# First layer of a four-layer image network: 64-row products on row halves, streamed weights, three PSUM double banks

## The chip, the cores and the metric

The kernel runs on one core of a Trainium2 chip. The metric is the device time in microseconds (us) of one execution. The core has a matrix engine (TensorE, in the profile PE, its weight loads PEld), a vector engine (DVE), a scalar engine (ACT), GpSimd (POOL) and a queue engine (SP) that here issues most DMAs.

## The reference

Four layers run one after the other on 8 images of 56 x 56 positions with 192 channels, all in fp32. The change touches the first, whose input is normalised in groups of 6 channels per image (as the kernel lays it out):

```
p = silu(x @ p_w.T + p_b);  q = silu(x @ q_w.T + q_b);  v = silu(x @ v_w.T + v_b)   # 192 -> 576
a1, a2 = rpe_mlp(...) * decay            # Toeplitz coefficients per channel, 2*56 each
qv = q * v
o1 = toeplitz(qv along w, a1);  o2 = toeplitz(qv along h, a2)
out = (p * (o1 + o2)) @ o_w.T + o_b      # 576 -> 192, then added to x
```

Per channel, o1 + o2 is computed as one product of two matrices with 120 rows: image rows beside a 56 x 56 Toeplitz table, for both directions at once. The other three layers (a window attention, a gated unit with attention and a recurrent scan) are the same before and after.

## The kernel before, in words

**Tiles.** In the first layer an image lies with its channels on the partitions: `xa` holds channels 0 to 127 (128 x 3136), and `xb` channels 128 to 191 of the upper half image on partitions 0 to 63 and of the lower half on 64 to 127 (128 x 1568). So every product over 192 channels is one product of 128 rows and one of 64; the 64-row products of the two halves use the two halves of the array's rows. `GroupNormSplit` (L79) measures an image with bn_stats (L115), spreads the means over groups by small products with a group matrix (L98, eight instructions) and settles scale and shift.

**Stages.** An image goes through five stages c = 0 to 4 of 128 channels (64 in the last). The lists of steps that a stage runs are woven together by `merge`, and the order of TensorE's instructions is exactly the order in which the program writes them (`manual_schedule` for PE); the other engines are put in order by the scheduler.

- `project` (L297, L304) computes q and v for the channels of the next stage in four groups of 14 rows. ACT applies silu (L313) and DVE and POOL write q*v twice into `qv`, straight and across (L325, L331).
- `turn_both` and `turn` (L358, L377) transpose `qv` channel rows; DVE copies the result into `ol` and ACT into `or` (L363, L384). A bank of PSUM is free when both have copied.
- `convolve` (L401) multiplies `ol` with `or` channel by channel, and results go to `ot` (L419, L421). Then `toeplitz` (L275) fetches the tables for the channels two steps on, over SP.
- `post` (after stages 1 and 3, run as the `fill` of stages 2 and 4) has seven groups of 8 image rows. `gate` computes p (L442 with 128 rows, L449 with 64) and its silu (L456). `back` transposes `ot` (L467, 120 rows at a time) and DVE multiplies with p (L476). `out` multiplies with o_w, 128 columns wide for the first 128 output channels (L487) and 64 wide for the rest (L492), and DVE adds to the accumulators `acca` and `accb` (L428, L430). `in_turn` runs them as back(g-1), gate(g), out(g-1).
- `post_tail` (fill of the next image's stage 0) does the same for the last 64 channels (L532, L539, L553, L559, L566, L578).
- In stages 0, 2 and 4 the fill runs with the turns; in stages 1 and 3 (and in stage 0 of the first image), which have no fill, the first two projection groups of the next stage do. So three and four turns follow each other there.

**Buffers.** PSUM has eight banks; the first layer uses them as four tiles of two banks, tag "c", in rotation. SBUF work tiles are "s" (128 x 784, four) and "po" (four). The weights of `project` and `post` (`wqv`, `wp`) stay in SBUF for the whole layer.

An fp32 product shows as two MATMUL records, a transposition as one. The form "64*128" in a record gives the rows and columns of the array that it uses.

Of the kernel before, what the change touches and what calls it, by code (L numbers as in the profile page):

```python
# [15 lines left out]
C = 192  # L16
CP = 96
# [36 lines left out]
HH, HQ = H // 2, HW // 2  # L54

# [17 lines left out]

def sub(ap, *dims):

    return bass.AP(ap.tensor, ap.offset, [list(ap.ap[0]), *(list(d) for d in dims)])


class GroupNormSplit:  # L79


    def __init__(self, cx, es, gmat):
        self.cx = cx
        nc = cx.nc
        pool = es.enter_context(cx.tc.tile_pool(name="gs_c", bufs=1))
        self.g = cx.tile(pool, [128, 2, 2, 128], "gmat")
        nc.sync.dma_start(self.g, gmat)
        self.eps = cx.tile(pool, [128, 1], "eps")
        nc.vector.memset(self.eps, EPS)
        self.small = es.enter_context(cx.tc.tile_pool(name="gs_s", bufs=1))  # L90

    def spread(self, bank, v):

        nc = self.cx.nc
        ps = bank()[:, 0:2]
        for m in range(2):
            for k in range(2):
                nc.tensor.matmul(  # L98
                    ps[:, m : m + 1], self.g[:, k, m, :], v[:, k : k + 1], start=(k == 0), stop=(k == 1)
                )  # L100
        return ps

    def steps(self, xa, xb):
# [4 lines left out]
        new = lambda name: cx.tile(self.small, [128, 2], name)  # L108
        mv = cx.tile(self.small, [128, 2, 2], "mv")
        mean, gms, dev = new("mean"), new("gms"), new("dev")  # L110
        parts = [(x, n, cx.tile(self.small, [128, n, 6], f"st{n}")) for x, n in ((xa, 7), (xb, 4))]
# [5 lines left out]
        def deviate(bank):  # L117
            for k, (_, _, st) in enumerate(parts):
                nc.vector.bn_aggr(mv[:, k, :], st.rearrange("p a b -> p (a b)"))
            nc.vector.tensor_copy(mean, mv[:, :, 0])  # L120
            nc.vector.tensor_copy(gms, self.spread(bank, mean))
            nc.vector.tensor_tensor(dev, mean, gms, ALU.subtract)
            nc.vector.tensor_tensor(dev, dev, dev, ALU.mult)
            nc.vector.tensor_tensor(dev, dev, mv[:, :, 1], ALU.add)

        def settle(bank):
            sd, rstd, nbias = new("sd"), new("rstd"), new("nbias")
            nc.scalar.activation(sd, self.spread(bank, dev), AF.Sqrt, bias=self.eps)
# [7 lines left out]
def layer0(cx, xin, xout, w, consts):  # L136
# [11 lines left out]
    T2, T1 = slice(0, H), slice(64, 64 + H)  # L148
    cx.open(B)
    cx.between = ExitStack()  # L150
    with ExitStack() as es:
        gn = GroupNormSplit(cx, cx.between, w["gmat"])
# [3 lines left out]
        wk = es.enter_context(tc.tile_pool(name="l0w", bufs=4))  # L156
        psc = es.enter_context(tc.tile_pool(name="l0a", bufs=4, space=PSUM))
# [4 lines left out]
        def bank():  # L162
            return banks()[:, 0]

        def load_raw(b):
            xa, xb = cx.tile(np_, [CA, HW], "xa"), cx.tile(np_, [128, HQ], "xb")
            image_dma(nc.sync, xin[b], xa, xb)
            return xa, xb
# [5 lines left out]
        wqv = [cx.tile(cp, [128, 9, 128], f"wqv{k}") for k in range(2)]  # L174
        wp = [cx.tile(cp, [128, NC, 128], f"wp{k}") for k in range(2)]
        for k in range(2):
            nc.scalar.dma_start(wqv[k], w[f"w_qv{k}"])
# [62 lines left out]
        for k in range(2):  # L240
            nc.scalar.dma_start(wp[k], w[f"w_p{k}"])
# [41 lines left out]
        def project(xn, c):  # L283


            n = 7 * H
            tail = c == NC - 1
# [4 lines left out]
            def gates(g):  # L292
                pss = [banks() for _ in js]
                for j, ps in zip(js, pss):
                    for h in range(2):
                        at = h * HQ + g * n
                        nc.tensor.matmul(  # L297
                            ps[:, h, 0:n], wqv[0][:, j, :], xn[0][:, at : at + n],
                            start=True, stop=False,
                        )  # L300
                for j, ps in zip(js, pss):
                    for h in range(2):
                        rows = slice(h * CB, (h + 1) * CB)
                        nc.tensor.matmul(  # L304
                            ps[:, h, 0:n], wqv[1][rows, j, :], xn[1][rows, g * n : (g + 1) * n],
                            start=False, stop=True,
                        )
                ts = []
                for i in range(2):
                    j, ps = js[0 if tail else i], pss[0 if tail else i]  # L310
                    rows = slice(i * DS, (i + 1) * DS) if tail else slice(0, 128)
                    t = cx.tile(wk, [128, 2, n], "s")[0 : DS if tail else 128]
# [119 lines left out]
        def post(j, xn, ot, acc):  # L432

            n = 4 * H

            def gate(g):
                ps = banks()
                out = lambda u, h: ps[:, h, u * n : (u + 1) * n]
                for u in range(2):
                    for h in range(2):  # L440
                        at = h * HQ + g * n
                        nc.tensor.matmul(  # L442
                            out(u, h), wp[0][:, 2 * j + u, :], xn[0][:, at : at + n],
                            start=(u == 0), stop=True, skip_group_check=True,
                        )
                for u in range(2):
                    for h in range(2):
                        rows = slice(h * CB, (h + 1) * CB)
                        nc.tensor.matmul(  # L449
                            out(u, h), wp[1][rows, 2 * j + u, :], xn[1][rows, g * n : (g + 1) * n],  # L450
                            start=False, stop=True, skip_group_check=True,
                        )
                sps = []
                for u in range(2):
                    sp = cx.tile(wk, [128, 2, n], "s")
                    nc.scalar.activation(  # L456
                        sp, ps[:, :, u * n : (u + 1) * n], AF.Silu,
                        bias=bp[:, 2 * j + u : 2 * j + u + 1],
                    )
                    sps.append(sp)  # L460
                return sps

            def back(g, sps):
                pt = banks()
                for h in range(2):
                    for i in range(4):
                        nc.tensor.transpose(  # L467
                            pt[:, h, i * 120 : (i + 1) * 120],
                            ot[:, :, h * HH + 4 * g + i],
                            ident[0:120, 0:120],  # L470
                        )
                pos = []
                for u in range(2):
                    po = cx.tile(wk, [128, 2, 4, H], "po")
                    src = pt[:, :, 0:480].rearrange("p h (i c) -> p h i c", c=120)
                    nc.vector.tensor_tensor(  # L476
                        po, sps[u].rearrange("p h (i c) -> p h i c", c=H),
                        src[:, :, :, u * 64 : u * 64 + H], ALU.mult,
                    )
                    pos.append(po.rearrange("p h i c -> p h (i c)"))  # L480
                return pos

            def out(g, pos):
                ps = banks()
                pa, pb = ps[:, 0, 0 : 2 * n].rearrange("p (h i) -> p h i", h=2), ps[:, 1, 0:n]
                for u in range(2):
                    nc.tensor.matmul(  # L487
                        pa, wo[:, 2 * j + u, 0:CA], pos[u], start=(u == 0), stop=(u == 1)
                    )
                for u in range(2):  # L490
                    for h in range(2):
                        nc.tensor.matmul(  # L492
                            pb[h * CB : (h + 1) * CB], wo[:, 2 * j + u, CA:], pos[u][:, h, :],
                            start=(u == 0), stop=(u == 1), skip_group_check=True,
                        )
                xv = acc[0].rearrange("p (h c) -> p h c", h=2)[:, :, g * n : (g + 1) * n]
                add(0, j, xv, pa)
                add(1, j, acc[1][:, g * n : (g + 1) * n], pb)

            return in_turn(gate, back, out, 7)  # L500

        def in_turn(gate, back, out, n):


            state = {}

            def turned(g):
                state[g] = back(g, state[g])

            def step(g):  # L510
                if g:
                    turned(g - 1)
                state[g] = gate(g)
                if g:
                    out(g - 1, state.pop(g - 1))

            last = [lambda: turned(n - 1), lambda: out(n - 1, state.pop(n - 1))]
            return [lambda g=g: step(g) for g in range(n)] + last

        def post_tail(xn, ot, acc):  # L520
# [7 lines left out]
            def gate(g):  # L528
                ps = banks()
                for h in range(2):  # L530
                    for p in range(2):
                        nc.tensor.matmul(  # L532
                            ps[sides[p], h, 0:n], wp[0][:, NC - 1, 0:DS],
                            rows(xn[0], h * 14 + g * 7, p),
                            start=True, stop=False, skip_group_check=True,
                        )
                for p in range(2):
                    for h in range(2):
                        nc.tensor.matmul(  # L539
# [1583 lines left out]
```

## Time and profile before

| what | value |
|---|---|
| device time, median of 3 runs | 4149.71 us (4142.44 to 4158.66) |
| span of the profiled execution | 4160.9 us |
| first layer in it | 0 to about 2024 us, 242 us for an image |
| PE busy in image 580 to 822 us | 234.12 of 242 us |
| DVE, ACT, POOL busy in it | 145.89, 99.28, 71.02 us |
| mean share of DMA engines in it | 0.36 |
| L297, L304 (project), means | 511, 518 ns |
| L442, L449 (gate of post), means | 358, 376 ns |
| L467 (back of post), mean | 287 ns |
| L487, L492 (out of post), means | 565, 365 ns |
| copies of a turn, L363: DVE ol, ACT or | 1207, 1008 ns |

No time outside the span is given for the profiled execution, so its span stands for its own time. A mean of a matmul contains its passage through the array, which overlaps with the next one's; how fast they follow one another is read from their starts in the timeline. "xN" counts records. Behind "idle" stands how long the engine waited before such instructions, and for what.

### The profile page before, as it was taken

The numbers are of one execution on the slowest core, as the hardware profiler recorded it, in microseconds if no ns is written. First come the engines' busy times: TensorE is split into PE (matmuls) and PEld (weight loads), VectorE is DVE, ScalarE is ACT, GpSimd is POOL, SyncE is SP. The second block draws the span as 40 slices with busy tenths as digits, with TensorE's granted clock in tenths as the row PEclk, the third lists the DMA queues.
The fourth block names the chain that finished last, engine by engine and source line by source line (L and its number), as shares of the span: only waits on it lengthen the run. The fifth ranks groups of instructions, "written<-read, shape, count | busy, mean of one in ns | idle before, by whom it ended". The sixth has DMA issues, their size and how long they took to land. (4 is left out here: it accounts for less than half of the span.)

```text
span 4160.9 us, 106559 instructions
## 1 busy us (share of the span) xinstructions
PE 3928.9 (94%) x46380; PEld 2544.2 (61%) x46380; DVE 2399.7 (58%) x3408; ACT 1778.2 (43%) x2021; POOL 1535.5 (37%) x1325
## 2 busy tenths in 40 slices
PE   6989999999999999999799999899998999998997
PEld 4666656666665666666466666544444555556997
DVE  5547566565755656565534444475566666665654
ACT  2334444344443434443234434243435555554664
POOL 3223232223322222242333333243334444444776
PEclk9999999999999999999899999999999999999999
DMA  7656242242624224241334444456648766653333
GB/s 152 137 109 149 63 117 63 80 101 63 148 64 117 63 69 111 63 121 52 103 78 105 101 107 109 121 177 190 185 142 198 179 160 160 157 138 106 90 104 96
DMA packets 380967, 483.55 MB, mean 116 GB/s; under 512 B 175444, under 2 KB 325236, under 8 KB 379108
## 3 DMA queue, kind: packets, MB, share of 16 engines
q1 hardware_dynamic: 376181, 469.62, 44.7%
q8 instruction: 365, 5.98, 0.6%
q10 hardware_dynamic: 3279, 4.13, 0.3%
q0 software_dynamic: 1040, 2.99, 0.3%
q14 instruction: 102, 0.84, 0.1%
HBM read 320.90 MB, written 155.65 MB: 115 GB/s over the span
## 5 line engine op out<-in xcount | busy, mean ns | idle before, releaser
L331 POOL TENSOR_TENSOR qv<-s,s 128x392 f32<-128x392 f32 (+3 forms) x320 | 579.1, 1836 | 1372.5 <-ACT s L313 1139.6
L297 PE MATMUL c<-xa,wqv 128*128 128x392 f32 x1152 | 426.4, 511 | 21.3 <-ACT or L363 13.6
L313 ACT ACTIVATE s<-c,bqv 128x784 f32<-128x784 f32 (+1 forms) x320 | 278.6, 911 | 354.5 <-PE c L304 201.0
L363 DVE COPY ol<-c 56x1024 f32<-56x1024 f32 x224 | 262.5, 1207 | 138.4 <-PE c L358 138.4
L325 DVE TENSOR_TENSOR qv<-s,s 128x784 f32<-128x784 f32 (+1 forms) x160 | 248.0, 1561 | 150.0 <-ACT s L313 150.0
L363 ACT COPY or<-c 56x1024 f32<-56x1024 f32 x224 | 222.7, 1008 | 240.1 <-DVE ol L363 230.3
L297 PEld LDWEIGHTS c<-xa,wqv 128*128 128x128 f32 x1152 | 206.7, 191 | 184.5 <-issue 33.9
L401 PEld LDWEIGHTS c<-or,ol 120*64 120x64 f32 x9216 | 276.9, 139 | 39.4 <-issue 31.7
L401 PE MATMUL c<-or,ol 120*64 120x56 f32 x9216 | 283.7, 224 | 15.7 <-DMA ol<-ed 7.8
L456 ACT ACTIVATE s<-c,bp 128x448 f32<-128x448 f32 x224 | 129.9, 631 | 248.5 <-PE c L449 248.4
L304 PE MATMUL c<-xb,wqv 64*128 64x392 f32 x1152 | 232.9, 518 | 0.0
L1987 POOL TENSOR_TENSOR y<-y,s 128x448 f32<-128x448 f32 x168 | 185.0, 1101 | 93.7 <-ACT s L1966 93.7
L1455 ACT ACTIVATE vb<-sm 128x1024 f32<-128x1024 f32 (+1 forms) x100 | 103.9, 1040 | 262.6 <-issue 224.1
L1956 PE MATMUL h<-ringv,am 128*64 128x57 f32 (+1 forms) x4400 | 192.8, 235 | 20.3 <-DVE ringv L1943 12.9
L487 PE MATMUL c<-po,wo 128*128 128x448 f32 x448 | 198.1, 564 | 10.8 <-DVE po L476 10.8
L1444 PE MATMUL v<-wvb,wa 128*128 128x512 f32 (+1 forms) x400 | 191.5, 611 | 4.0 <-ACT wa L1330 3.6
L430 DVE TENSOR_TENSOR acca<-c,acca 128x392 f32<-128x392 f32 (+1 forms) x120 | 67.2, 585 | 221.4 <-PE c L492 204.4
L1956 PE MATMUL h<-ringh,am 128*64 128x57 f32 (+1 forms) x4400 | 186.3, 232 | 8.4 <-DVE ringh L1962 8.4
L442 PE MATMUL c<-xa,wp 128*128 128x224 f32 x896 | 191.9, 357 | 0.0
L1956 PEld LDWEIGHTS h<-ringv,am 128*64 128x64 f32 x4400 | 168.3, 140 | 23.7 <-DVE ringv L1943 13.9
L963 PE MATMUL c<-wv,xc 128*126 128x192 f32 x896 | 175.4, 339 | 0.2 <-ACT v L973 0.2
L304 PEld LDWEIGHTS c<-xb,wqv 64*128 64x128 f32 x1152 | 97.7, 186 | 124.0 <-issue 89.3
(242 smaller groups left out, 7735.7 us busy)
## 6 DMA issues: line engine op xcount, KB each, us to landing
or<-tt SPq DMA_DIRECT2D x252, 196.0 KB
ol<-tt SPq DMA_DIRECT2D x252, 196.0 KB
vt<-v SPq DMA_DIRECT2D x56, 672.0 KB
v<-vb SPq DMA_DIRECT2D x96, 384.0 KB
x<-x SPq DMA_DIRECT2D x110, 168.0 KB
x<-x SPq DMA_DIRECT2D x110, 112.0 KB
bs<-bt SPq DMA_DIRECT2D x48, 256.0 KB
bs<-bs SPq DMA_DIRECT2D x54, 224.0 KB
```

The lines of the kernel that those rows point to most:

```text
L297: nc.tensor.matmul(ps[:, h, 0:n], wqv[0][:, j, :], xn[0][:, at : at + n], start=True, stop=False,)
L304: nc.tensor.matmul(ps[:, h, 0:n], wqv[1][rows, j, :], xn[1][rows, g * n : (g + 1) * n], start=False, stop=True,)
L313: nc.scalar.activation(t, ps[rows, :, 0:n], AF.Silu, bias=bqv[rows, j : j + 1])
L325: nc.vector.tensor_tensor(sub(qv[rows, 7 * g :, 64 + H - 1 :], (HH * 120, 2), (120, 7), (-1, H)), *(t.rearrange("p u (h w) -> p u h w", w= ...
L331: eng.tensor_tensor(sub(qv[rows, w0:, H - 1 - 7 * g - HH * u :], (120, w1 - w0), (-1, 7)), *(t[:, u].rearrange("p (h w) -> p w h", w=H)[:, ...
L363: copy(dst[:, :, :, i0 : i0 + 8], view[rows])
L401: nc.tensor.matmul(ps[u * 64 : (u + 1) * 64, k, v * H : (v + 1) * H], left[:, d * H : d * H + 64], right[:, d * H : (d + 1) * H], start=Tr ...
L442: nc.tensor.matmul(out(u, h), wp[0][:, 2 * j + u, :], xn[0][:, at : at + n], start=(u == 0), stop=True, skip_group_check=True,)
L487: nc.tensor.matmul(pa, wo[:, 2 * j + u, 0:CA], pos[u], start=(u == 0), stop=(u == 1))
L1444: nc.tensor.matmul(out, x[:, at : at + n], wt, start=(k == 0), stop=(k == 1), skip_group_check=True,)
L1956: nc.tensor.matmul(ps[sides[c], y], am[a][:, m * CB : (m + 1) * CB], old[:, x], start=(n < 2), stop=True, skip_group_check=True,)
L1987: nc.gpsimd.tensor_tensor(v, v, line[:, j], ALU.add)
```

## The change

The image is loaded as three chunks of 64 channels, each with the upper half image on partitions 0 to 63 and the lower on 64 to 127 (`halves_dma`, 16 transfers for 12). Every product over 192 channels becomes three pairs of 64-row products, where the two of a pair use the two halves of the array's rows and write two different PSUM banks. `back` transposes the two 56-row halves of `ot` separately. `out` for the first 128 channels gathers two groups in a PSUM tile "o" of its own and runs in two rounds, so that the row halves never write one bank together: first each half to its bank, then swapped; `seen`, a copy of four numbers, stands between them. The last, single group goes with 128 rows (`alone`). The sum into `acca` comes once for two groups, and so does `rest`, which makes the other 64 channels. The tail makes its gates first, then backs, outs and rests. PSUM has three tiles "c" and one "o" instead of four "c"; SBUF has six "s" of 128 x 896. The weights of `project` and `post` are fetched per stage. The group norm of an image in three chunks uses a matrix of seven blocks, and `spread` makes its products in row halves into two banks and adds them on DVE.

```diff
-        wk = es.enter_context(tc.tile_pool(name="l0w", bufs=4))
-        psc = es.enter_context(tc.tile_pool(name="l0a", bufs=4, space=PSUM))
+        wk = es.enter_context(tc.tile_pool(name="l0w", bufs=6))
+        psc = es.enter_context(tc.tile_pool(name="l0a", bufs=3, space=PSUM))
...
+        def work(*shape):
+            n = int(np.prod(shape))
+            t = cx.tile(wk, [128, 4 * 4 * H], "s")[:, 0:n]
+            return t.rearrange("p (a b) -> p a b", a=shape[0])
...
         def load_raw(b):
-            xa, xb = cx.tile(np_, [CA, HW], "xa"), cx.tile(np_, [128, HQ], "xb")
-            image_dma(nc.sync, xin[b], xa, xb)
-            return xa, xb
+            x = cx.tile(np_, [128, 3, HQ], "x")
+            halves_dma(nc.sync, xin[b], x)
+            return x
...
+        def fetch_wqv(q, queue=nc.sync):
+            if q < B * NC:
+                wqv[q] = cx.tile(cp, [128, 3, 2, 128], "wqv", bufs=2)
+                queue.dma_start(wqv[q], w["w_qv"][q % NC])
+
+        def fetch_wp(j, queue=nc.sync):
+            wps[j] = cx.tile(cp, [128, 3, 2, 128], "wp")
+            queue.dma_start(wps[j], w["w_p"][j])
...
     def spread(self, bank, v):
...
+        sides = [slice(0, 128)] if whole else [slice(0, CB), slice(CB, 128)]
+        for m in range(n):
+            ks = [k for k, to in pairs if to == m]
+            for k in ks:
+                for r, rows in enumerate(sides):
+                    nc.tensor.matmul(
+                        ps[:, m : m + 1] if whole else ps[:, r, m : m + 1],
+                        g[rows, pairs.index((k, m)), :], v[rows, k : k + 1],
+                        start=(k == ks[0]), stop=(k == ks[-1]), skip_group_check=True,
+                    )
...
+            nc.vector.tensor_copy(out, ps[:, 0, 0:n])
+            nc.vector.tensor_tensor(out, ps[:, 1, 0:n], out, ALU.add)
...
             def gates(g):
-                pss = [banks() for _ in js]
...
+                for i in range(len(js)):
+                    ps = banks()
+                    for k in range(3):
+                        for h, rows in enumerate(halves):
+                            nc.tensor.matmul(
+                                ps[:, h, 0:n], wqv[q][rows, k, i, :],
+                                xn[rows, k, g * n : (g + 1) * n],
+                                start=(k == 0), stop=(k == 2),
+                            )
+                    pss.append(ps)
...
         def post(j, xn, ot, acc):
...
+            groups = [(0, 1), (2, 3), (4, 5), (6,)]
...
             def gate(g):
                 ps = banks()
                 for u in range(2):
...
+                    for k in range(3):
+                        for h, rows in enumerate(halves):
+                            nc.tensor.matmul(
+                                ps[:, h, u * n : (u + 1) * n], wps[j][rows, k, u, :],
+                                xn[rows, k, g * n : (g + 1) * n],
...
+            def back(g):
                 pt = banks()
                 for h in range(2):
                     for i in range(4):
-                        nc.tensor.transpose(
-                            pt[:, h, i * 120 : (i + 1) * 120],
-                            ot[:, :, h * HH + 4 * g + i],
-                            ident[0:120, 0:120],
-                        )
...
+                        at = (4 * h + i) * H
+                        for u, rows in enumerate((T2, T1)):
+                            nc.tensor.transpose(
+                                pt[:, u, at : at + H], ot[rows, :, h * HH + 4 * g + i],
+                                ident[rows, rows],
+                            )
+                sp = gated[g]
+                nc.vector.tensor_tensor(sp, sp, pt[:, :, 0 : 2 * n], ALU.mult)
+
+            def out(q, swap):
+                if not swap:
+                    outs[q] = cx.tile(psc, [128, 2, 512], "o", bufs=1)
+                for i, g in enumerate(groups[q]):
+                    for u in range(2):
+                        for r, rows in enumerate(halves):
+                            h = r ^ swap
+                            nc.tensor.matmul(
+                                outs[q][:, h, i * n : (i + 1) * n], wo[rows, 2 * j + u, 0:CA],
+                                gated[g][rows, u, h * n : (h + 1) * n],
+                                start=(i == 0 and u == 0 and not swap), stop=True,
+                                skip_group_check=True,
+                            )
+                if not swap:
+                    seen = cx.tile(gn.small, [1, 2, 2], "seen")
+                    nc.vector.tensor_copy(seen, outs[q][0:1, :, 0 : n + 1 : n])
+                else:
...
+                    add(0, j, xv, outs.pop(q)[:, :, 0:m])
...
+            def rest(q):
+                ps = banks()[:, 0]
...
+            def alone(g):
+                pa = banks()[:, 0, 0 : 2 * n]
...
+            def one(q):
+                if q > 1:
+                    out(q - 2, 1)
+                gate(2 * q)
+                if q < 3:
+                    back(2 * q)
+
+            def two(q):
+                if q:
+                    out(q - 1, 0)
+                if q < 3:
+                    gate(2 * q + 1)
+                    back(2 * q + 1)
+                    if q:
+                        rest(q - 1)
+                else:
+                    back(6)
+
+            def end():
+                rest(2)
+                rest(3)
+                alone(6)
+                out(2, 1)
+
+            return [lambda f=f, q=q: f(q) for q in range(4) for f in (one, two)] + [end]
...
+            steps = [lambda f=f, g=g: f(g) for f in (back, out) for g in range(2)]
+            return [gates, *steps, lambda: (rest(0), rest(1))]
...
+                i = b * NC + c
+                fetch_wqv(i + 2)
+                ahead = project(xn if two else nxt, i + 1) if two or more else []
...
+                if fill:
+                    fetch_wp({2: 1, 4: 2, 0: 0}[c])
```

## The prediction, made before the changed kernel was run

> **What bounds the kernel now.** I read the page first, its busy shares and slices:
>
> ```profile
> PE 3928.9 (94%) x46380; PEld 2544.2 (61%) x46380; DVE 2399.7 (58%) x3408; ACT 1778.2 (43%) x2021; POOL 1535.5 (37%) x1325
> PE   6989999999999999999799999899998999998997
> ```
>
> TensorE is busy in nearly every slice; the first layer is the first 19 or so of 40 (its last matmul starts at 2022 us). Next the busy time by stretches for one image (580 to 822), then its second projection stage, the first `post`, a gates stage, and the tail:
>
> ```profile
> 580.00:822.00 242.00, 234.12 (x2570) 157.64 (x2564) 145.89 (x184) 99.28 (x119) 71.02 (x40) 1.00 0.36 91
> 605.98:638.57 32.59, 31.16 (x474) 22.12 (x471) 23.91 (x27) 17.29 (x19) 15.20 (x8) 1.00 0.47 118
> 638.57:686.67 48.10, 47.62 (x368) 33.18 (x365) 21.80 (x33) 17.32 (x23) 0.00 (x0) 1.00 0.28 59
> 805.98:825.85 19.87, 17.04 (x210) 9.11 (x207) 16.77 (x24) 8.67 (x9) 0.43 (x1) 0.91 0.63 180
> ```
>
> The columns are length, then busy PE, weight loads, DVE, ACT, POOL, clock, DMA. An image takes 242 us, PE works in 234; only in the tail is DVE (16.77) its equal. A busy PE need not stream, so I read the timeline of one `post` step:
>
> ```profile
> 1993.37 1.15 PE L467 MATMUL c<-ident,ot 120*128 120x120 f32 x8
> 1994.35 1.69 PE L442 MATMUL c<-xa,wp 128*128 128x224 f32 x8
> 1995.97 1.03 PE L449 MATMUL c<-xb,wp 64*128 64x224 f32 x8
> 1996.92 1.77 PE L487 MATMUL c<-po,wo 128*128 128x448 f32 x4
> 1998.62 0.98 PE L492 MATMUL c<-po,wo 128*64 128x224 f32 x8
> ```
>
> The first number is the start: 0.98, 1.62, 0.95 and 1.70 us from group to group. Single starts in the trace split this: L442's follow each other by 189 ns, L449's come in pairs 7 ns apart, a pair every 189; but the last L442 to the first L449 takes 283, and the first L449 pair to the second 286. So each change of the rows*columns form costs about 190 ns, once for running empty, once for exposed weights. Into L492 (64 columns) it is about 145. The step has 4 changes, 5 with a turn (L358, 64*120) in it.
>
> **What the skill says.** TensorEngine Tiling (Array Packing), Key Properties: changing the tiling mode drains TensorE. The trace agrees, 190 ns. The same page, PSUM Bottleneck: tiling speeds TensorE, not the emptying of PSUM. The trace shows it where turns come in a burst, below. TensorE: Matmul & The Clock Gate, Part 3: matmuls in different row groups start about 4 ns apart and run together; here 7. Its Part 2 (LDWEIGHTS) has a weight load take columns / 1.2 ns, 107 for 128, whatever the rows. L467 (120 rows) comes every 111, but L553 (56 rows, 128 columns) every 62: the trace has 64-row loads faster.
>
> **The change, part by part.** Products first, in steady intervals. A projection group is now 8 full products of 329 ns plus 4 pairs of 329, 3.95 us, plus two changes: 4.35 measured. New: 12 pairs of 329, 3.95. A gate: 8 x 189 + 4 pairs x 189 = 2.27; new 12 pairs, 2.27. Output: 4 x 376 + 4 pairs x 189 = 2.26; new 8 pairs + 4 pairs, 2.27. The halves win nothing in products. Backward transpositions: 8 x 111 = 0.89; new 8 pairs. I price a pair at L553's 62, because L358's pairs (59.5) take no longer than L377's single ones (59): 0.50; the other end is 111 a pair, 0.89, no gain (44 us in all).
>
> Changes of form: in the built order of instructions the first layer has 973 before and 232 after, 741 fewer at some 185 ns: 137 us. With 112 x 0.39 = 44 for the transpositions, 181 us if no wait came up.
>
> But PSUM falls from four double banks to three, plus one for the outputs. So I go by stages, with the copies of the trace.
>
> Each `post`: 7 x (2.27 + 2.26 + 0.89 + 0.47 for a turn) = 41.2, measured 48.1: 34 changes and 0.6 of waits. New: 7 x (2.27 + 2.27 + 0.50 + 0.47) = 38.6, plus 8 changes 1.4, plus 1.0 for waits: 41.0. Gain 7.1, twice an image. Is the third bank enough? A turn's bank is wanted by `rest` 4.3 us later (output 1.5, gate 2.3, back 0.5). DVE's product of 896 elements (0.96 for 784 at L559, so 1.08), then the ol copy 1.2, then ACT's or copy 1.0 and hand-overs end about 3.9 after it. It holds, by 0.4. The single output tile needs its DVE sum (about 1.15) within 3.2 us: it holds. The small copy `seen` makes DVE wait for half an output; the product and a turn's copy queue behind it, but PE asks for the second half 5 us later. Costed at nothing.
>
> The gates of stages 0 and 4 (17.39 each, timeline 825.85 to 843.24): 4 x 0.4 saved, gain 1.55 each.
>
> Stage 1, where turns come in bursts:
>
> ```profile
> 610.91 1.58 PE L358 MATMUL c<-ident,qv 64*120 64x64 f32 x48
> 611.58 3.48 DVE L363 COPY ol<-c 56x1024 f32<-56x1024 f32 x3 [5.56 <-PE c L358]
> 612.42 3.05 PE L297 MATMUL c<-xa,wqv 128*128 128x392 f32 x8
> 612.83 3.27 ACT L363 COPY or<-c 56x1024 f32<-56x1024 f32 x3 [0.60 <-DVE ol L363]
> 619.81 2.90 PE L297 MATMUL c<-xa,wqv 128*128 128x392 f32 x8 [0.89 <-ACT or L363]
> ```
>
> The two copies of a bank follow each other, so the first turn's bank is free at 613.85. Four banks back, the gate at 612.42 needs another one; three back it needs this one and waits 1.4. The last turn of the next four then waits for the first of them, 1.35, the gates after it 0.5: some 3.5 of waits where there is 1.0. From 610.91 to the end of those gates I get 15.0 against 13.25. Then `spread`: 8 instructions of 112 ns become 28 or 16, in pairs; between 62 and 112 a pair, 0.5 to 1.6 us, about as now. DVE adds the two halves behind it in a chain whose steps take up to 1.5 beside POOL, so the second spread is 0.5 later. The stage loses 2.15. Stage 3, same way: its burst ends 1.0 later, its gates save 0.7, net +0.3. Stage 2's gates hold two spreads: +0.5.
>
> The tail: DVE's work in it (seven ol copies of 1.2, two products, twelve sums of 0.52, three statistics of 0.6 queued among them) is unchanged, and with three banks PE follows it: 21.3 by hand against 19.87, +1.4. The last tail, without turns, loses its waits, -2.
>
> DMA: per stage 393 KB of weights, on SP. A projection's fetch has its buffer free a stage ahead; one for gates waits on PE for the gates of the `post` just done, and only transfers wanted later queue behind it. 16 loads of an image for 12, and 459 KB for the new group matrix ahead of the first image: +1.5 at the start (0 to 4).
>
> Sum per image: -14.2 - 3.1 + 2.15 + 0.3 + 0.5 + 1.4 = -12.95; eight images -103.6; at the ends (no gates after the last image, its tail, the start) +1. About -102. The profiled span is 4160.9, so 4059; this execution is 11 us above the median of the runs, 4149.7, which gives 4048.
>
> **Rivals.** A: the third bank costs nothing in bursts and tail, as copies fit the later order; then the bare count holds, -181: 3969. For it: PE waits only some 8 us of 242 now. Against it: the copies' chain of 2.2 per bank. C: weights of unbroken pairs are not hidden as they are in runs of four pairs. For it: the first layer's trace has no run of more than four such pairs except transpositions. Against: 329 and 189 already stand in the second to fourth pair. 20 ns on each of 3840 pairs is 77 us: 4125. B, slower: the margin of 0.4 in `post` isn't there, because DVE's queue sets another order, and each of 416 allocations (26 in 16 posts) waits. 0.25 us each cancels the gain, 0.30 gives 4173. Against it: DVE has 6.4 us of work (products 2.16, ol copies 2.4, sums 0.65 and 1.15) in the 11.3 of two groups. That the pairs don't run together is hardly open: L449 does exactly this.
>
> **Numbers.** Forecast 0.66, A 0.15, C 0.13, B 0.06. About 0.5% (21 us) is what a measurement can tell from no change. C lies at that bound, half on each side: faster 0.88, same 0.06, slower 0.06. The range, 3980 to 4120, leaves out most of A, the upper part of C, and B, about 0.2; the transpositions' other end (+44) and the waits' (-45 in stages 1 and 3) lie within it.
>
> **What would show it.** Right: `post` near 41 us, projection pairs at 329, transposition pairs near 62, gates of stage 0 near 15.9; PE waiting for ACT's or copy more often in stages 1 and 3. Wrong: waits of over 0.3 at each gate or turn in `post`; pairs spaced by over 340; a tail far from 21; or a first image held by its tables, which wait 7.8 us for DMA now.

## The result, and the profile after

The changed kernel takes 4137.7 us (median of 20 runs, 4128.4 to 4152.3) against 4149.6 us: a ratio of 0.9974, 95% interval 0.9964 to 0.9983, some 11 us faster. 4048 was forecast, 3980 to 4120 as its range. The first layer's last matmul gives way to the second layer's first at 2009.2 us of the profiled execution, against 2035.7; of those 26 us about 8 belong to that one execution before, whose first image took 39.2 us for stage 1; 31.5 us in experiment 2, which differs from it there in the layout of one tile.

The page of the changed kernel, busy shares and TensorE's slices:

```profile
PE 3833.4 (93%) x51036; PEld 2688.9 (65%) x51036; DVE 2387.0 (58%) x3318; ACT 1792.9 (43%) x2021; POOL 1512.5 (37%) x1325
PE   6998989999899999999799999899998999998997
```

4656 more matmuls (pairs in place of full products), 95 us less busy, and yet hardly less time. TensorE now pauses, as one image, its stage 1, its first `post` and a tail show by stretches (length, busy PE, weight loads, DVE, ACT, POOL, granted clock as a share of full speed, DMA share, GB/s):

```profile
546.90:792.90 246.00, 227.31 (x3160) 178.18 (x3156) 143.90 (x175) 102.52 (x119) 68.36 (x41) 0.98 0.41 103
595.66:630.83 35.17, 31.74 (x497) 23.19 (x497) 22.58 (x26) 16.84 (x18) 13.55 (x8) 0.95 0.33 82
630.83:675.75 44.92, 43.09 (x552) 39.47 (x550) 21.46 (x24) 17.35 (x23) 0.00 (x0) 1.00 0.34 73
792.90:814.14 21.24, 16.59 (x225) 9.52 (x221) 17.59 (x26) 8.67 (x9) 0.09 (x1) 0.92 0.75 200
```

Before, the image had 8 us without PE work, now 19. Stage 1 ran at a granted clock of 1.00 before, now at 0.95; experiments 7 and 9 come back to it. What PE waited for in the first layer, in us, times, and the longest ("issue" means that it waited for nothing that the profile shows):

```profile
PE c L408 <- ACT or L413: 28.9, 33, 1.2
PE c L408 <- ACT s L363: 17.2, 16, 1.1
PE c L352 <- ACT or L413: 16.6, 32, 1.4
PE c L451 <- issue: 12.0, 7, 2.9
PE c L451 <- DVE ot L471: 9.8, 8, 1.5
PE c L493 <- ACT s L500: 9.7, 8, 1.3
PE c L451 <- ACT s L363: 9.0, 7, 1.3
```

In the kernel before the waits for ACT's or copy came to 24.8 us and all waits between 100 and 1880 us to 71; now all come to 136. Two places show how. A burst of turns in stage 1:

```profile
600.39 3.48 DVE L413 COPY ol<-c 56x1024 f32<-56x1024 f32 x3 [8.54 <-PE c L408]
601.64 3.27 ACT L413 COPY or<-c 56x1024 f32<-56x1024 f32 x3 [0.73 <-DVE ol L413]
602.70 3.56 PE L352 MATMUL c<-x,wqv 64*128 64x392 f32 x20 [1.05 <-ACT or L413]
```

The first bank is taken at 600.39 by DVE, at 601.64 by ACT, and is free a little after 602.6: the gates behind the third turn need just this one. And the convolution behind stage 2's gates:

```profile
694.34 1.70 ACT L674 ACTIVATE x<-x,nbias,rstd 128x1568 f32<-128x1568 f32 x1 [2.44 <-DVE nbias L172]
696.06 1.28 ACT L363 ACT_TABLE_LOAD   x1
697.35 1.72 ACT L363 ACTIVATE s<-c,bqv 128x784 f32<-128x784 f32 x2
698.32 3.95 PE L451 MATMUL c<-or,ol 120*64 120x56 f32 x128 [1.30 <-ACT s L363]
```

The silu of the last gates (697.35) stands in ACT's queue behind the scaling of the next image and a table load. Until it has run, two of three banks are held; the convolution has used the third and stops for 1.30 us.

The steps of a `post`, from the timeline:

```profile
656.78 2.43 PE L493 MATMUL c<-x,wp 64*128 64x224 f32 x24
659.05 0.98 PE L512 MATMUL c<-ident,ot 56*128 56x56 f32 x16
659.96 1.73 PE L547 MATMUL c<-s,wo 128*64 128x224 f32 x16
661.63 0.69 PE L408 MATMUL c<-ident,qv 64*120 64x64 f32 x16
```

The gate takes its 2.27 us. The eight pairs of transpositions (L512) take 0.91 to the next group; at the priced 62 ns a pair they would take 0.50 and a change of form.

Cut at the first matmul of each stage, medians over images 2 to 7 of each trace (tail and stage 0: 2 to 8), in us (runs numbered as in the next section):

| kernel | tail, stage 0 | stage 1 | first post, stage 2 | stage 3 | second post, stage 4 | sum |
|---|---|---|---|---|---|---|
| before | 44.9 | 31.9 | 74.9 | 23.4 | 69.2 | 244.3 |
| forecast | 44.75 | 34.05 | 68.3 | 23.7 | 60.55 | 231.35 |
| changed | 46.5 | 35.2 | 74.6 | 24.5 | 62.5 | 243.3 |
| 1 contiguous `ot` | 47.3 | 35.4 | 73.3 | 23.8 | 60.5 | 240.3 |
| 3 ring of four | 43.6 | 32.8 | 70.8 | 23.0 | 62.8 | 233.0 |
| 4 run 3's order, ring of three | 46.0 | 35.3 | 75.3 | 23.8 | 63.3 | 243.7 |
| 5 before, ring of three | 47.4 | 34.3 | 77.3 | 24.4 | 70.1 | 253.5 |
| 6 contiguous, ring of four | 43.5 | 33.2 | 69.4 | 23.1 | 60.4 | 229.6 |
| 7 gates only, ring of four | 44.6 | 33.0 | 75.7 | 23.0 | 67.6 | 243.9 |

### The profile page after: what moved, and what is told of

It is laid out like the page before. It is cut to its first block, busy times and chain, and to the rows that moved or that the text cites. A ratio compares the mean times of both kernels' runs of the same rounds, so it can differ in the third digit from the quotient of the medians.

```text
span 4134.9 us, 115884 instructions
## 1 busy us (share of the span) xinstructions
PE 3833.4 (93%) x51036; PEld 2688.9 (65%) x51036; DVE 2387.0 (58%) x3318; ACT 1792.9 (43%) x2021; POOL 1512.5 (37%) x1325
## 4 chain that ended last, share of the span: by engine, by line
PE 69%; DVE 10%; issue 7%; ACT 5%; DMA 3%; POOL 3%; SPq 2%; ACTq 0%; DVEq 0%; POOLq 0%
PE c L352 12%; PE c L493 6%; PE v L1533 6%; PE h L2045 5%; PE c L451 4%; PE c L1052 4%; PE o L526 4%; PE y L1087 3%; PE kv L1593 3%; PE c L1058 2%; PE c L512 2%; PE c L1755 2%; DVE ol L413 2%; PE c L547 2%; DVE qv L375 1%
## 5 line engine op out<-in xcount | busy, mean ns | idle before, releaser
L381 POOL TENSOR_TENSOR qv<-s,s 128x392 f32<-128x392 f32 (+3 forms) x320 | 558.4, 1772 | 1373.9 <-ACT s L363 1073.7
L352 PE MATMUL c<-x,wqv 64*128 64x392 f32 x3456 | 609.6, 503 | 27.4 <-ACT or L413 18.2
L352 PEld LDWEIGHTS c<-x,wqv 64*128 64x128 f32 x3456 | 336.3, 190 | 246.0 <-ACT or L413 26.4
L363 ACT ACTIVATE s<-c,bqv 128x784 f32<-128x784 f32 (+1 forms) x320 | 291.4, 913 | 389.7 <-PE c L352 369.7
L375 DVE TENSOR_TENSOR qv<-s,s 128x784 f32<-128x784 f32 (+1 forms) x160 | 236.6, 1488 | 126.4 <-ACT s L363 126.2
L493 PE MATMUL c<-x,wp 64*128 64x224 f32 x2688 | 279.3, 352 | 9.7 <-ACT s L500 9.7
L517 DVE TENSOR_TENSOR s<-s,c 128x896 f32<-128x896 f32 x112 | 121.8, 1088 | 243.5 <-ACT s L500 219.9
L493 PEld LDWEIGHTS c<-x,wp 64*128 64x128 f32 x2688 | 252.8, 187 | 12.6 <-ACT s L500 10.8
L2045 PE MATMUL h<-ringv,am 128*64 128x57 f32 (+1 forms) x4400 | 192.0, 235 | 17.6 <-DVE ringv L2032 10.6
L408 PE MATMUL c<-ident,qv 64*120 64x64 f32 x3584 | 144.5, 223 | 49.7 <-ACT or L413 30.0
L408 PEld LDWEIGHTS c<-ident,qv 64*120 64x120 f32 x3584 | 127.5, 136 | 92.5 <-ACT or L413 45.1
```

The source lines that it names most:

```text
L352: nc.tensor.matmul(ps[:, h, 0:n], wqv[q][rows, k, i, :], xn[rows, k, g * n : (g + 1) * n], start=(k == 0), stop=(k == 2),)
L363: nc.scalar.activation(t, ps[rows, :, 0:n], AF.Silu, bias=bqv[rows, j : j + 1])
L375: nc.vector.tensor_tensor(sub(qv[rows, 7 * g :, 64 + H - 1 :], (HH * 120, 2), (120, 7), (-1, H)), *(t.rearrange("p u (h w) -> p u h w", w= ...
L381: eng.tensor_tensor(sub(qv[rows, w0:, H - 1 - 7 * g - HH * u :], (120, w1 - w0), (-1, 7)), *(t[:, u].rearrange("p (h w) -> p w h", w=H)[:, ...
L408: nc.tensor.transpose(view[:, k, :, i], qv[rows, i0 + i, :], ident[rows, rows])
L493: nc.tensor.matmul(ps[:, h, u * n : (u + 1) * n], wps[j][rows, k, u, :], xn[rows, k, g * n : (g + 1) * n], start=(u == 0 and k == 0), stop ...
```

## The experiments

The kernel before came to between 4149.6 and 4156.4 us from chip to chip, so ratios to it, on the same chip, are compared; "us" is the ratio's distance from 1 times 4150. "Clock" is TensorE's granted clock, the mean over all runs of a version; in the kernel before it was 0.983 to 0.984 beside every experiment.

| run | median us | ratio (95%) | us | clock |
|---|---|---|---|---|
| changed | 4137.7 | 0.9974 (0.9964 to 0.9983) | -11 | 0.9805 |
| 1 contiguous `ot` | 4119.1 | 0.9905 (0.9888 to 0.9923) | -39 | 0.981 |
| 2 before, contiguous `ot` | 4142.9 | 0.9971 (0.9960 to 0.9983) | -12 | 0.9836 |
| 3 ring of four | 4070.1 | 0.9784 (0.9764 to 0.9804) | -90 | 0.982 |
| 4 run 3's order, ring of three | 4153.6 | 0.9988 (0.9976 to 1.0001) | -5 | 0.9814 |
| 5 before, ring of three | 4235.5 | 1.0184 (1.0162 to 1.0206) | +76 | 0.980 |
| 6 contiguous, ring of four | 4038.4 | 0.9720 (0.9705 to 0.9734) | -116 | 0.9818 |
| 7 gates only, ring of four | 4143.0 | 0.9971 (0.9958 to 0.9984) | -12 | 0.9829 |
| 8 no streaming | 4137.4 | 0.9953 (0.9940 to 0.9967) | -20 | 0.9805 |
| 9 copies by bank | 4193.9 | 1.0100 (1.0085 to 1.0115) | +42 | 0.9755 |
| 10 run 6, copies by bank | 4091.3 | 0.9858 (0.9839 to 0.9877) | -59 | 0.9788 |
| 11 halved copies | 4092.4 | 0.9843 (0.9827 to 0.9860) | -65 | 0.9838 |
| 12 run 3, halved copies | 4047.5 | 0.9733 (0.9710 to 0.9755) | -111 | 0.9832 |

Two theories stood at the start: that the backward transpositions keep 111 ns because of the stride of their weights (rival: because pairs of 128-column loads can't run together), and that the third bank costs what the halves gain (rival: the order in the queues of DVE and ACT).

**1 and 2: the stride.**

```diff
-dst = ot[:, d0 : d0 + 16, :].rearrange("p (k v) h -> p k (v h)", k=2)
-src = ps[0:120, :, 0 : 8 * H]
+dst = ot[:, :, d0 : d0 + 16].rearrange("p h (k v) -> p h k v", k=2)
+src = ps[0:120, :, 0 : 8 * H].rearrange("p k (v h) -> p h k v", h=H)
-ot = cx.tile(cp, [120, 128, H] if two else [H, H, DS], "ot")
+ot = cx.tile(cp, [120, H, 128] if two else [H, H, DS], "ot")
-ot[rows, :, h * HH + 4 * g + i]
+ot[rows, h * HH + 4 * g + i, :]
```

> Only the layout of ot differs: row-major with the 128 channels innermost, so that the weights of the backward transpositions are read contiguously and the copies after the convolution write with a stride of 512 bytes. Theory (the stride of 224 bytes sets the 111 ns of a pair): pairs at about 62 ns, 896 pairs x 49 ns = 44 us less, some of it lost to waits: 4090 to 4105 us. Rival (two loads of 128 columns into the two row halves cannot run together): pairs stay at 111 ns and the time stays at 4138 within 6 us, or rises by up to 10 us if the strided copies are slower.

The weight loads of L512 in the changed kernel, then in run 1 (minimum, median, maximum in ns):

```profile
L512 PEld LDWEIGHTS c<-ident,ot x1792: 182/201/208, 137.9 to 1975.1; 56*128 56x128 f32 x200
```

```profile
L512 PEld LDWEIGHTS c<-ident,ot x1792: 134/138/143, 143.2 to 1952.4; 56*128 56x128 f32 x200
```

Two lines of run 1's timeline:

```profile
649.44 0.65 PE L512 MATMUL c<-ident,ot 56*128 56x56 f32 x16
650.02 1.73 PE L547 MATMUL c<-s,wo 128*64 128x224 f32 x16
```

A pair follows the last every 62.0 ns (110.6 in the changed kernel), and the group ends after 0.58. The theory holds and the rival falls: two row halves load together. The size was missed in part: the median group is 0.33 us shorter (0.49 against 0.82 where no change of form follows), 37.5 us over 112 groups and not 44; the device time fell by 28. The rest came up as waits; in the first `post` the gates now wait twice for ACT (14.4 us in the layer, 9.7 in the changed kernel).

In the kernel before, the same layout:

```diff
-ot[:, :, h * HH + 4 * g + i]
+ot[:, h * HH + 4 * g + i, :]
```

> The kernel before with ot row-major (contiguous weights for its 120-row transpositions), nothing else. Theory (stride, not pairing, set the pace of the changed kernel's pairs; here the 120 columns that stream through, 101 ns at the 1.19 columns per ns of the other products, bound it too): 111 falls to about 101 ns, 896 x 10 = 9 us less, 4141 of 4150 at most. Rival (the stride alone makes the load long and the stream hides nothing): down to 62 ns, 40 us less.

The transpositions of 120 rows fell from 111 to 102.5 ns, with loads of 140 in place of 198: the theory. This layout alone, in the kernel before, wins as much as the whole change did.

**3 to 6: the bank.** Run 3 takes the output from the ring; the output's first half then has to come later, or its own release would stand behind what needs it.

```diff
-psc = es.enter_context(tc.tile_pool(name="l0a", bufs=3, space=PSUM))
+psc = es.enter_context(tc.tile_pool(name="l0a", bufs=4, space=PSUM))
-    outs[q] = cx.tile(psc, [128, 2, 512], "o", bufs=1)
+    outs[q] = banks()
 def two(q):
-    if q:
-        out(q - 1, 0)
     if q < 3:
         gate(2 * q + 1)
         back(2 * q + 1)
-        if q:
-            rest(q - 1)
     else:
         back(6)
+    if q:
+        out(q - 1, 0)
+    if 0 < q < 3:
+        rest(q - 1)
 def end():
     rest(2)
+    out(2, 1)
     rest(3)
     alone(6)
-    out(2, 1)
```

> The output tile of the pairs is taken from the common ring, which so has four double banks again; to make that possible the first half of an output follows the gates and the transposition of its step instead of preceding them (about three more changes of form in a post, 16 x 3 x 0.19 = 9 us more). Theory (the waits that came up, some 65 us of idle TensorE in the first layer, come from the third bank in place of the fourth): idle time goes back towards 75 us, 35 to 55 us less: 4083 to 4103 us. Rival (they come from the order of the copies in the queues of DVE and ACT): 4138 to 4150 us.

It gained more than the theory had it: 79 us by the ratios. Waits that are left of those above:

```profile
PE c L408 <- ACT s L363: 9.9, 9, 1.2
PE c L408 <- ACT or L413: 9.7, 7, 1.4
PE c L352 <- ACT or L413: 8.6, 16, 0.7
```

Those of the convolution for DVE's ot and ACT's s and of the gate in `post` are gone. Run 4 is the control: the order of run 3 (the edits of `two` and `end` alone) with three banks and "o".

> The control to the common ring of four: its order of the output's halves (after the gates and the transposition of their step), but the banks of the changed kernel, three in the ring and one for the output. Theory (the 68 us of that run come from the bank): the extra changes of form remain and the waits too, 4138 to 4152 us. Rival (they come from the later place of the output): 4070 to 4095 us.

By the ratios the order alone costs 6 us (the intervals touch); so the bank is worth 85 us in that order. And in the kernel before:

```diff
-psc = es.enter_context(tc.tile_pool(name="l0a", bufs=4, space=PSUM))
+psc = es.enter_context(tc.tile_pool(name="l0a", bufs=3, space=PSUM))
```

> The kernel before with three double banks of PSUM in place of four, nothing else. Theory (the lost bank costs what the halves gain): 45 to 65 us slower than before, 4195 to 4215 us, with the waits in the bursts of turns, the convolution behind the gates and the tail. Rival (three banks are enough in the kernel before, and the waits of the changed kernel come from its own order): within 12 us of 4150.

76 us slower, more than expected; the same waits come up in it (L297, L358 and L442 are the gates, turns and `post` gates there):

```profile
PE c L297 <- ACT or L363: 18.6, 38, 0.9
PE c L358 <- ACT s L313: 17.7, 18, 1.1
PE c L442 <- ACT s L456: 7.3, 7, 1.0
```

Three comparisons (79, 85 and 76 us) in different orders agree on the price of a bank. The rival falls. The price isn't made of waits alone: from stage 1 of the first image to that of the last, run 3 is 70 us shorter than the changed kernel, and 46 of these are waits of TensorE (85 against 131) and up to 12 the granted clock, of which more under 7 and 9; the rest stands in neither. Run 6 has the edits of 1 and 3 together:

> Both edits at once: contiguous ot and the output tile in the common ring of four. Theory (in the run with contiguous ot alone, half of the 43.5 us that the pairs gained went into waits for the third bank; with four banks those waits are gone): the whole 40 to 44 us come on top of the run with four banks, 4026 to 4032 us at its 4070. Rival (the posts are by then held by the copies and products of DVE and ACT, however many banks there are): 20 to 25 us, 4045 to 4050 us.

27 us come on top by the ratios (32 by the medians), between the two expectations: the `post` of stage 4 took 2.4 us an image, all that seven groups have to give, that of stage 2 1.4. At 4038.4 us it is the fastest version, 2.8% below the kernel before.

**7: what the halves gain, and where.** Run 7 has the changed kernel's projections and gates, and `back` and `out` of the kernel before:

```diff
-wk = es.enter_context(tc.tile_pool(name="l0w", bufs=6))
-psc = es.enter_context(tc.tile_pool(name="l0a", bufs=3, space=PSUM))
+wk = es.enter_context(tc.tile_pool(name="l0w", bufs=4))
+psc = es.enter_context(tc.tile_pool(name="l0a", bufs=4, space=PSUM))
...
-def back(g):
+def back(g, sps):
...
-def out(q, swap):
+def out(g, pos):
...
-return [lambda f=f, q=q: f(q) for q in range(4) for f in (one, two)] + [end]
+return in_turn(gate, back, out, 7)
```

> Only the projections and the gates work on the row halves; the transpositions back (120 rows) and the output (128 rows, one group at a time) are those of the kernel before, so that no bank goes to the output and the ring has four. Its posts keep four changes of form a step as before; the projections lose theirs: 19 of them an image, 4 groups in most, at 0.4 us a group, some 55 to 60 us in all. Theory (the part of the change that needs no bank gains, the part that takes one gives it back): 4090 to 4105 us, faster than the full change. Rival (the posts' changes of form are the larger part and the bank is cheap): above 4138.

The theory fell: 12 us, not 55. Stage 4 gained the 1.6 us that its four groups should. In stage 2 the longer `spread` takes 2.4 back (75.7 against 74.9 less 1.6). In stage 0 the tail and the gates gained 2.8 us (34.2 against 37.0), but the convolution behind them lost 2.9 (10.6 against 7.7), largely in waits for issue of 1.1 to 3.0 us. Stage 1 holds the other pair of spreads (the waits for DVE's dev rose from 3.8 to 7.7 us) and got 1.1 longer by the median, but not by its own work: in four of the images 2 to 7 the trace has stretches of 3.4 us and more in it at half the granted clock. Image 5 has none, image 6 has one:

```profile
1082.00:1113.46 31.46, 29.63 (x499) 24.16 (x498) 23.32 (x26) 17.43 (x19) 15.69 (x8) 1.00 0.45 116
1325.50:1358.70 33.20, 31.38 (x499) 23.82 (x498) 23.25 (x26) 17.43 (x19) 15.63 (x8) 0.94 0.48 105
```

The same 499 records take 1.7 us more. Without such a stretch stage 1 takes 31.2 to 31.5 us, against 31.9 before: its gates did gain, and the gain was lost again. From run 7 to run 3 the `post`s change (and the number of work tiles in SBUF): 78 us, 4.9 us in each (47.8 and 47.7 to 42.9). What reaches the device time is nearly all from the `post`s, where four changes of form a step had stood, and the output needs the bank there.

**8: streaming.** Run 8 leaves out the later fetches of weights and uses the first ones throughout.

```diff
 def fetch_wqv(q, queue=nc.sync):
     if q < B * NC:
+        if q > 1:
+            wqv[q] = wqv[q - 2]
+            return
         wqv[q] = cx.tile(cp, [128, 3, 2, 128], "wqv", bufs=2)
...
 def fetch_wp(j, queue=nc.sync):
+    if wps:
+        wps[j] = wps[0]
+        return
     wps[j] = cx.tile(cp, [128, 3, 2, 128], "wp")
```

> The changed kernel with the weights of the first two projections and of the first gates used for all: the later fetches of weights are left out (the values are then those of other layers' columns, the work is the same). Theory (the streamed weights land behind other work): within 6 us of 4138. Rival (they hold back the loads of the tables, of x or of instructions): 15 to 40 us less.

4137.4 against 4137.7 by the medians, 9 us by the ratios, whose intervals touch. It isn't what holds the kernel back; the waits for issue stay too (16.7 us, 17.6 in the changed kernel).

**9 to 12: how long a bank is held.**

```diff
-for t, rows, copy in zip(both, (T2, T1), (nc.vector.tensor_copy, nc.scalar.copy)):
-    dst = t[rows, :, 0:ND].rearrange("p k (d i) -> p k d i", i=H)
-    copy(dst[:, :, :, i0 : i0 + 8], view[rows])
+for k, copy in enumerate((nc.vector.tensor_copy, nc.scalar.copy)):
+    for t, rows in zip(both, (T2, T1)):
+        dst = t[rows, k, 0:ND].rearrange("p (d i) -> p d i", i=H)
+        copy(dst[:, :, i0 : i0 + 8], view[rows, k])
```

> The changed kernel, its three banks left, with the copies behind the turns of two heads split by bank instead of by rows: DVE copies the first bank of a double bank, ACT the second, each in two copies of 512 elements in place of one of 1024. They no longer follow each other, so that a double bank is held for some 1.2 us (two copies of about 0.6) in place of 2.2. Theory (the lost bank costs what the time that a bank is held makes it cost): the waits of turns and gates for ACT's or copy in the bursts and the tail (28.9 + 16.6 + 4.1 us) fall by more than half, 25 to 40 us less: 4098 to 4113 us. Rival (the number of banks alone counts, or DVE and ACT have no room): within 10 us of 4138.

It became 52 us slower than the changed kernel. The timeline of run 9 says why:

```profile
613.63 0.68 DVE L414 COPY ol<-c 56x512 f32<-56x512 f32 x1 [7.27 <-PE c L408]
614.32 0.69 DVE L414 COPY or<-c 56x512 f32<-56x512 f32 x1
615.11 0.58 ACT L414 COPY ol<-c 56x512 f32<-56x512 f32 x1 [0.97 <-DVE or L414]
615.70 0.58 ACT L414 COPY or<-c 56x512 f32<-56x512 f32 x1
616.33 0.93 PE L352 MATMUL c<-x,wqv 64*128 64x392 f32 x4 [1.45 <-ACT or L414]
```

ACT still waits for DVE; the built program has that wait although the two no longer share a bank. So the hold grew from 2.25 to 2.65 us in 224 such turns, and the run tested the theory the other way round. The 52 us aren't the price of the hold alone, however. From stage 1 of the first image to that of the last, the changed kernel and run 9:

```profile
101.21:1811.25 1710.04, 1577.84 (x22065) 1240.58 (x22062) 1009.79 (x1197) 714.87 (x830) 484.74 (x280) 0.99 0.45 110
103.60:1859.20 1755.60, 1601.03 (x22064) 1255.49 (x22060) 1053.08 (x1394) 746.67 (x1026) 483.53 (x280) 0.97 0.44 107
```

Of the 45.6 us more, 21 are waits (152 against 131). The trace has 95.6 us at half the granted clock in this stretch against 47.8, which accounts for up to 24 more. Over all runs the clock was 0.9755 against 0.9805. Whether the longer pauses bring the lower clock with them, no run separates.

> Contiguous ot, the output tile in the common ring of four, and the copies behind the turns split by bank. Theory of the holding time: the waits for ACT's or copy left with four banks (9.7 + 8.6 + 6.8 + 5.4 + 4.6 + 3.4 us) go for the most part, 15 to 30 us less than the 4038 without the split. Rival (with four banks the copies are off the path, the split only adds fixed cost): 4035 to 4050 us.

57 us slower than run 6: in the same stretch the waits rose from 85 to 117 us, so with four banks too the chain of the copies is on the path, and the time at half clock from 37.5 to 71.7. Both expectations missed. Next the hold is shortened, by leaving out half of the columns:

```diff
-copy(dst[:, :, :, i0 : i0 + 8], view[rows])
+copy(dst[:, :, :, i0 : i0 + 4], view[rows, :, :, 0:4])
```

> The changed kernel with three banks; the copies behind the turns of two heads leave out half of their columns (512 elements in place of 1024; TensorE's work is whole, half of the turned values are missing), so that a double bank is held for some 1.3 us in place of 2.25. Theory (a bank fewer costs what it does because the two copies hold a bank so long): the waits for ACT's or copy (28.9 + 16.6 + 4.1 us) and part of those on ACT's s (17) go, 40 to 70 us less than 4138. Rival (the number of banks and the order of the queues, not the holding time): within 15 us of 4138.

54 us less than the changed kernel by the ratios, as the theory has it; the waits of turns and gates for ACT's or copy fall to 4.2 and 6.6 us. The clock rose too, from 0.9805 to 0.9838: up to 14 of the 54 us.

> The same halved copies with the output tile in the common ring of four. Theory of the holding time: less is left to win, 20 to 40 us below the 4070 of this ring with whole copies, so that four banks are then worth under 45 us over three (68 with whole copies). Rival: what the copies cost does not depend on the banks; both fall alike and the distance stays at 60 us or more.

21 us less than run 3. The bank is then worth 46 us in place of 79, just past the expected bound. So halving the turns' copies takes away two fifths of the bank's price. It shortens the hold of a bank and the queues of DVE and ACT alike (DVE's ol copies fall from 264 to 149 us), and no run separates the two. The rest doesn't depend on these copies (waits for ACT's s at 17.2 and 9.2 us and for ot at 8.3 us stay in run 11).

## Why the prediction was wrong, step by step

- **Products, right.** Intervals in the trace after: 329 ns a pair in `project`, 189 in gates and outputs, in runs of up to 48 pairs. No gain and no loss; rival C (weights not hidden in long runs) is out.
- **Changes of form, right in the `post`s.** There 4.9 us are gained at four banks with transpositions at 111 ns; by the forecast's own terms without their gain 4.4. Gates of stage 4: 15.9 us, as forecast. But what the gates gained hardly reached the device time (run 7: 12 us): waits for issue in stage 0, stretches at half clock in stage 1 and the longer spread of stage 2 took it back.
- **Backward transpositions, wrong.** "I price a pair at L553's 62, because L358's pairs take no longer than L377's single ones": all three read contiguous weights, L467 and the new L512 read theirs 224 bytes apart. 110.6 ns were measured, the other end. The trace of before had told it: L467's loads took 198 ns, those of L553 139. The Trainium skill has the rule, in SBUF — State Buffer, Door 1: The DMA port swizzle, the note on cachelines: lines of 16 bytes, so that fp32 may be strided by up to 4 elements for free. The trace agrees (201 ns with a stride of 56 elements, 138 without); no run tests strides near 4. Size: 28 us (run 1 against the changed kernel).
- **The third bank, mis-sized.** Stage by stage the forecast gave it some 5.7 us an image (stage 1's burst 2.5, stage 3's 1.0, tail 1.4, `post`s 0.8), 46 us; it is 10.3 (table, changed against run 3), 79 us. Stage 1's burst was sized rightly (2.4; 2.5 forecast), stage 3's nearly (1.5; 1.0). The tail came out near the forecast (20.9 us, 21.3 forecast) partly by luck: the forecast added 1.4 for the bank and nothing for the new order, but with four banks the tail takes 18.3 against 19.6 before, so the order gains 1.3 and the bank costs 2.6. The most is in stage 2, 3.8 us where 0.4 was forecast. What was not followed failed there: the convolution behind stage 2's gates (waits of 2.5 us, where ACT's queue holds the silu back), and "it holds, by 0.4" for the first `post`, whose second gate waits 1.3 us for ACT. Size: 33 us. The Trainium skill's TensorEngine Tiling (Array Packing), PSUM Bottleneck, was cited for it: tiling speeds up TensorE and not the emptying of PSUM. That is borne out in part. With four banks the waits rise from 70 to 85 us; but the kernel before, without the change, pays 76 us for a bank too.
- **Not in the forecast: waits for issue.** 17.6 us between 100 and 1880 us against 5.4 (0.3 in run 2). They stay with four banks (12.8 us in run 3) and without streaming (run 8), so neither is their cause. In the first layer ten of them last over 0.4 us, and after each PE goes on 1.3 to 1.6 us after the end of a 16 KB block of the queue of kind "instruction", as at 595.66 after 594.31, 842.86 after 841.36 and 1079.63 after 1078.32; such blocks come 9.7 us apart on average. The same holds for all such waits of runs 1, 3, 6, 7 and 8. 36 more such blocks go with the 9312 more loads and matmuls. That TensorE ran out of instructions fits all of this, but no run changes the instructions alone to test it. Size: 12 us.
- **Not in the forecast: the granted clock.** 0.9805 over the 20 runs of the changed kernel, 0.983 to 0.984 in the kernel before. That is an estimated 11 us of full-speed time (4138 x 0.0195 less 4150 x 0.0167); 7 of them come back with the fourth bank (0.982 in run 3) and so lie in the bank's 79.
- **Spread and start.** The pairs took 112 ns, within the bounds given; in stage 2 the net +0.5 forecast is +0.8 in run 7. TensorE reaches stage 1 of the first image at 101.2 us, 2.3 later than before; 1.5 was forecast. Stage 1's terms as written (1.75 and 0.5) add up to 2.25, not to 2.15; that is 1 us in all.

28, 33 and 12 make 73 of the 90 us missed; of the remaining 17 the clock may hold 3 or 4, and the others are not attributed. The waits came neither evenly (rival B) nor not at all (A). The range left out what it should have held: the transpositions' other end (44) lay in it, but for the bank it allowed only for fewer waits (-45), and B, the dear bank, lay outside.

## What to carry to other kernels

When a change takes a PSUM bank, price it as a change of its own: follow every stage's allocations around the ring with the queues of the engines that empty them, or build the kernel before with one bank fewer and measure that. A row of the profile prices another operation only if its operands lie alike; compare the durations of the loads before taking a neighbour's interval. Ahead of a faster TensorE, shorten what holds its banks. And compare the granted clocks of two versions before their difference is put down to a wait.

## What was not expected of the hardware

- A 128-column fp32 weight load for a transposition takes 138 ns contiguous and 201 ns with a stride of 224 bytes, at 56 rows; 140 and 198 at 120 rows. Pairs on the two row halves then follow every 62 and 110.6 ns.
- The copies into `ot` were no slower for the other layout, in which they read PSUM 224 bytes apart and write 16 channels in a row: 905 ns on ACT in both, 1076 and 1079 on DVE (run 1).
- Double banks held 0.4 us longer in 224 turns (run 9) cost 52 us, though DVE is busy for 58% of the span and ACT for 43% in the changed kernel. In the profiled executions about half of it shows as waits and about half as time at half clock.
- The granted clock drops to half in stretches of 3.4 us or a multiple of it, not at the same places in every image and run. One of them made a stage of 31.46 us 1.7 us longer (run 7).
- The copies' chain (DVE, then ACT) was not broken here. The Trainium skill, PSUM — Partial Sum Buffer, "PSUM bank collisions raise a hardware error", has two engines collide in the same bank and quadrant of 32 partitions only, and the copies use partitions 0 to 55 and 64 to 119; no run here lets them go at once.
